# Layer norm statistics from narrow matmuls of raw tokens and of their squares, in a hybrid scan, attention and expert kernel

## The chip, the core and the metric

The kernel runs on one core of a Trainium2 chip. The metric is the device time of one execution in microseconds (us); for a kernel it is the median of several runs. A profiled execution also has a span, from the first instruction to the last. The engines are PE (TensorE: matmuls; PEld is its loading of weights), DVE (VectorE), ACT (ScalarE), POOL (GpSimd) and SP, which issues the DMAs. Everything is float32. In the profile a float32 matmul shows as two records, so 24 records are 12 matmuls of the program.

## What is computed

The input is four images of 384 channels and 32 x 32 pixels. Layer 0 is a group norm, a selective scan in four directions, a layer norm over channels and a GELU, added to the image. Layer 1 takes the 1024 pixels as tokens: a layer norm, causal attention with one head, then a layer norm and a gated mixture of four experts, of which each token uses two, each added to its input.

```python
x = x + _L0_conv_ref(_gn(x), ...)
t = _to_tokens(x)
t = t + _L1_attn_ref(_ln_t(t), Wq, Wk, Wv)
t = t + _L1_ffn_ref(_ln_t(t), gate_w, gate_b, w1, b1, w2, b2)
...
def _ln_t(v, eps=1e-5):
    m = jnp.mean(v, axis=-1, keepdims=True)
    s = jnp.var(v, axis=-1, keepdims=True)
    return (v - m) / jnp.sqrt(s + eps)
```

The norm at the end of `_L0_conv_ref` is the same over channels, with a weight and a bias, and a GELU after it.

## The kernel before

Tokens lie along the free dimension, channels on the 128 partitions in three blocks (M = 3). So a mean over channels is a matmul with `mean_w`, a matrix filled with 1/384, and its result has one number per token.

**Ticks.** The order of all instructions is written out by the program itself, in ticks. There are 768 of them for the scans (192 an image): tick t does the decay (`decay`, an Exp on ACT), the product v (`front`, L561 on DVE), the scan (`middle`, L567 on DVE), the product with C (`back`, L584 on POOL) and, every fourth tick, 16 records of y matmuls on PE (`row`, L609). In the first image many of the v products come from PE instead. `evict` (L629) takes y out of PSUM when 64 ticks of a channel block are done, into `yb`.

**Fillers.** Beside the scans of image b+1 the program places what is left of image b. `finish` (the layer norm named `l0_b`, a GELU at L888, the residual addition at L893) and `ready` (the layer norms `ff_b_0` and `ff_b_1`, one for each half of 512 tokens, and the gates) run from the list `side`; the attention and the experts (`ph`, L1272, and `fy`, L1297; L1306 and L1309 scale and add an expert's output) run from the list `waiting`. These are generators. Each `yield "pe", n` says that matmuls worth about n us were just issued; `go_on` gives the fillers 3.3 of that per tick while experts run and 4.4 while attention runs, a side generator at most until its budget of 1.0 is used up in that tick. `yield "wait", n` lets n ticks pass; `yield "inner"` resumes in the next tick but between v and the scan. What isn't issued by the last tick of the scans runs behind them. The last image's attention and experts have no scan beside them.

**Buffers.** Four PSUM banks (`banks`) and eight SBUF slots of 4 KB a partition (`slots`) are shared by all fillers; `take` waits for ticks until one is free.

**The layer norm** (`layernorm(dst, src, name, lag)`, from L639) works on n blocks of 512 tokens: n = 2 for `l0_b`, where dst and src are the same tile, n = 1 for `ff_b_h`. There are 4 of the former and 8 of the latter in a run. Its steps:

- L652: three matmuls of 128x128 by 512 for a block put the mean, repeated on all partitions, into a bank `mu`.
- L660: DVE subtracts it from the three channel blocks (128 x 1536) into dst.
- L672: ACT squares dst into three slots `sq`.
- L679: narrow matmuls (32 columns, four side by side with `tile_position`) sum the squares into the bank `var`, each group of 128 tokens on its own 32 partitions.
- L687, L692: ACT's root, then DVE's reciprocal on the narrow result `rs`.
- L698: four matmuls a block spread the narrow rows back over all partitions, into a bank `rb`.
- L708: DVE multiplies dst by it.

The attention's own norm, `scaled_tokens` (L900), has the narrow form already: raw tokens and squares go through narrow matmuls (L914), ACT squares the mean (L923), DVE subtracts (L925), then root and reciprocal (L927, L929); since its weights are centred beforehand (`fold`), only the root is spread and applied.

Of the kernel before, what the change touches and what calls it, by code (L numbers as in the profile page):

```python
# [8 lines left out]
F32 = mybir.dt.float32  # L9
AF = mybir.ActivationFunctionType  # L10
ALU = mybir.AluOpType
# [4 lines left out]
P = 128  # L16
B = 4
C = 384
M = C // P
# [30 lines left out]
def hybrid_kernel(  # L50
# [22 lines left out]
    nc = tc.nc  # L73
# [4 lines left out]
    one = ctx.enter_context(tc.tile_pool(name="one", bufs=1))  # L78
# [34 lines left out]
    inner = {}  # L113
# [4 lines left out]
    class Shared:  # L118
# [20 lines left out]
        def give(self, *names):  # L139
# [3 lines left out]
    banks = Shared(  # L143
        FIRST_BANKS,
        lambda i, name: (ps_m if i < FIRST_BANKS else pools["pm"]).tile(
            [P, 512], F32, tag=f"pm{i}", name=name
        ),
        0,
    )
    slots = Shared(  # L150
        SLOTS, lambda i, name, *shape: slotp.tile(list(shape), F32, tag=f"s{i}", name=name), 1
    )
# [7 lines left out]
    ident = const.tile([P, P], F32, tag="ident", name="ident")  # L160
    make_identity(nc, ident)
    mean_w = const.tile([P, P], F32, tag="mean_w", name="mean_w")
    nc.vector.memset(mean_w, 1.0 / C)
    eps = const.tile([P, 1], F32, tag="eps", name="eps")
# [474 lines left out]
    def layernorm(dst, src, name, lag):  # L639

        width = src.shape[2]
        n = width // 512
        mus = []
        for h in range(n):
            mu = yield from banks.take(f"mu_{name}_{h}")  # L650
            for c in range(M):
                nc.tensor.matmul(  # L652
                    mu, mean_w, src[:, c, bass.ts(h, 512)], start=(c == 0), stop=(c == M - 1)
                )
            mus.append(mu)
            yield "pe", 2.6
        yield "inner", 0
        for h in range(n):
            s = bass.ts(h, 512)
            nc.vector.tensor_tensor(  # L660
                dst[:, :, s], src[:, :, s], mus[h].unsqueeze(1).to_broadcast([P, M, 512]),
                ALU.subtract,
            )
            banks.give(f"mu_{name}_{h}")
        sqs = []
        for c in range(M):
            sq = yield from slots.take(f"sq_{name}_{c}", P, width)
            sqs.append(sq)
        for h in range(n):
            for c in range(M):  # L670
                s = bass.ts(h, 512)
                nc.scalar.activation(sqs[c][:, s], dst[:, c, s], AF.Square)  # L672
        yield "wait", lag
        var = yield from banks.take(f"var_{name}")
        for h in range(n):
            for c in range(M):
                for q in range(4):
                    o = h * 512 + q * P
                    nc.tensor.matmul(  # L679
                        var[32 * q : 32 * (q + 1), h * P : (h + 1) * P], mean_w[:, :32],  # L680
                        sqs[c][:, o : o + P], start=(c == 0), stop=(c == M - 1),
                        tile_position=(0, 32 * q),
                    )
            yield "pe", 1.0
        slots.give(*[f"sq_{name}_{c}" for c in range(M)])
        rs = one.tile([P, n, P], F32, tag=f"rs{n}", name=f"rs_{name}")
        nc.scalar.activation(  # L687
            rs, var[:, : n * P].rearrange("p (h t) -> p h t", t=P), AF.Sqrt, bias=eps
        )
        banks.give(f"var_{name}")  # L690
        yield "wait", 1
        nc.vector.reciprocal(rs, rs)  # L692
        yield "wait", lag
        backs = []
        for h in range(n):
            spread_ = yield from banks.take(f"rb_{name}_{h}")
            for q in range(4):
                nc.tensor.matmul(  # L698
                    spread_[:, q * P : (q + 1) * P],
                    ident[:, 32 * q : 32 * q + 1].to_broadcast([P, P]), rs[:, h, :],  # L700
                    start=True, stop=True,
                )
            backs.append(spread_)
            yield "pe", 1.0
        yield "inner", 0
        for h in range(n):
            s = bass.ts(h, 512)
            nc.vector.tensor_tensor(  # L708
                dst[:, :, s], dst[:, :, s], backs[h].unsqueeze(1).to_broadcast([P, M, 512]),
                ALU.mult,  # L710
            )
            banks.give(f"rb_{name}_{h}")

    folded = []

# [162 lines left out]
    def finish(b):  # L878

        yb = ybs[b]  # L880
        yield from layernorm(yb, yb, f"l0_{b}", 0)
        xrs = []
        for m in range(M):
            xr = yield from slots.take(f"xr_{b}_{m}", P, L)
            nc.sync.dma_start(xr, x[b, m * P : (m + 1) * P, :])
            xrs.append(xr)
        for m in range(M):
            nc.scalar.activation(  # L888
                yb[:, m, :], yb[:, m, :], AF.Gelu, bias=lnb[:, m : m + 1], scale=lnw[:, m : m + 1]
            )  # L890

            def add(m=m, xr=xrs[m]):
                nc.vector.tensor_add(yb[:, m, :], xr, yb[:, m, :])  # L893
                slots.give(f"xr_{b}_{m}")
                if m == M - 1:
                    finished.add(b)

            defer(1 + m // 2, add)
# [282 lines left out]
    def ready(b, h, xn, src=None):  # L1181

        if src is None:
            nc.sync.dma_start(xn, t2_d[b][:, :, bass.ts(h, 512)])
            src = xn
            yield "wait", 2
        yield from layernorm(xn, src, f"ff_{b}_{h}", 1)
        yield "wait", 1
        normed.add((b, h))
        yield from gates(b, h, xn)  # L1190
        gated.add((b, h))
# [212 lines left out]
    t = 0  # L1404
# [86 lines left out]
```

## Time and profile before

| | |
|---|---|
| median of 5 runs | 3751.58 us (3750.2 to 3755.34) |
| the profiled execution | 3754.29 us, span 3752.1 us |
| PE busy | 3356.3 us (89%) |
| DVE busy | 2961.4 us (79%) |
| ACT busy | 2086.5 us (56%) |
| POOL busy | 1817.8 us (48%) |
| mean granted TensorE clock | 0.929 |

| group | count | busy us | mean ns |
|---|---|---|---|
| L652 PE, mu of l0 | 48 | 21.7 | 594 |
| L652 PE, mu of ff | 48 | 22.3 | 596 to 601 |
| L660 DVE, subtract, both | 16 | 27.7 | 1740 to 1756 |
| L679 PE, var of l0 and ff | 384 | 14.2 | 275 to 292 |
| L698 PE, spread of l0 and ff | 128 | 19.1 | 296 to 301 |
| L708 DVE, multiply, both | 16 | 27.7 | 1746 to 1748 |
| L567 DVE, scan | 768 | 1749.2 | 2283 |
| L561 DVE, v | 664 | 841.4 | 1267 |

Matmuls are pipelined: the mean of one record is longer than the distance to the next (a 512-column record follows another after 0.43 us), and a busy PE is not PE at its peak. A wait is idle time of an engine before an instruction, put down to the instruction that released it. The clock is the share of full speed that TensorE was granted.

Three phases can be told apart. Up to 691 us the scans of image 0 run with few fillers. From there to 3098 us the scans of images 1 to 3 run with the fillers of images 0 to 2 beside them. From 3098 us on there are only the last image's norm, attention and experts, and a rest of image 2's.

### The profile page before, as it was taken

Reading aid. Unit: us, or ns where it says so; the run is one execution under the profiler, and the core shown is the slowest. Engines: PE = TensorE matmul, PEld = TensorE weight load, DVE = VectorE, ACT = ScalarE, POOL = GpSimd, SP = SyncE. Lnnn points to the kernel's source line nnn. Section 1 sums busy time; section 2 is a strip of 40 time slices with the busy share of each in tenths; the row PEclk is TensorE's granted clock in tenths of the full one; section 3 lists DMA queues with packets and bytes.
Section 4 is the critical chain, followed back from the end, with each engine's and each line's share of the span. In section 5 each row is a group of like instructions: output and inputs, shape, how many; then the busy total and the mean of one; then the engine's idle time right before and its main releaser. Section 6 shows DMA issues by size and latency. Waiting matters only on the chain. (4 is left out here: it accounts for less than half of the span.)

```text
span 3752.1 us, 35189 instructions
## 1 busy us (share of the span) xinstructions
PE 3356.3 (89%) x11891; PEld 1533.1 (41%) x11891; DVE 2961.4 (79%) x2084; ACT 2086.5 (56%) x2832; POOL 1817.8 (48%) x776
## 2 busy tenths in 40 slices
PE   4676666789999999899999999789999998999999
PEld 1333333345343343345333344354444444544444
DVE  5899899988999998989998999999999982210000
ACT  5788888556666555556655555455554552412121
POOL 2677777555565565545555665455665650000000
PEclk7777877889999999899999999999999999999999
DMA  6565555645665766436666655455656551322321
GB/s 207 211 235 198 205 210 214 227 151 191 226 228 199 256 211 232 162 137 215 225 216 231 206 203 198 145 185 185 223 191 240 181 180 38 92 79 85 95 81 53
DMA packets 408019, 680.03 MB, mean 181 GB/s; under 512 B 33520, under 2 KB 279968, under 8 KB 407840
## 3 DMA queue, kind: packets, MB, share of 16 engines
q1 hardware_dynamic: 401632, 677.40, 52.6%
q8 instruction: 94, 1.54, 0.2%
q10 hardware_dynamic: 6208, 0.39, 0.1%
q14 instruction: 85, 0.70, 0.1%
HBM read 605.16 MB, written 72.55 MB: 181 GB/s over the span
## 5 line engine op out<-in xcount | busy, mean ns | idle before, releaser
L584 POOL TENSOR_TENSOR h<-h,bc 128x1024 f32<-128x1024 f32 x768 | 1816.7, 2370 | 1270.4 <-DVE v L561 1123.3
L567 DVE TENSOR_TENSOR_SCAN h<-da,v 128x1024 f32<-128x1024 f32 x768 | 1749.2, 2283 | 56.4 <-PE v L872 25.8
L554 ACT ACTIVATE da<-dt,a 128x1024 f32<-128x1024 f32 x768 | 887.1, 1163 | 864.2 <-DVE h L567 765.1
L1297 PE MATMUL fy<-ht,w 128*128 128x512 f32 x2304 | 1022.5, 601 | 7.6 <-ACT ht L1261 5.9
L1272 PE MATMUL ph<-fx,w 128*128 128x512 f32 x2304 | 1019.6, 598 | 2.0 <-ACT dt L433 0.9
L561 DVE TENSOR_TENSOR v<-du,bc 128x1024 f32<-128x1024 f32 x664 | 841.4, 1267 | 63.0 <-DMA du<-dts 20.0
L1297 PEld LDWEIGHTS fy<-ht,w 128*128 128x128 f32 x2304 | 436.6, 192 | 581.2 <-issue 551.7
L1272 PEld LDWEIGHTS ph<-fx,w 128*128 128x128 f32 x2304 | 434.1, 191 | 578.7 <-issue 533.3
L609 PE MATMUL y<-h,sel 128*32 128x512 f32 x3072 | 496.6, 666 | 93.8 <-POOL h L584 91.8
L1257 ACT ACTIVATE ht<-ph,b1s 128x512 f32<-128x512 f32 x384 | 258.2, 680 | 479.6 <-PE ph L1272 478.1
L1306 DVE SCALAR_TENSOR_TENSOR fy<-fy,b2s,tw 128x512 f32<-128x512 f32 x96 | 72.1, 751 | 424.4 <-PE fy L1297 424.4
L609 PEld LDWEIGHTS y<-h,sel 128*32 128x32 f32 x3072 | 98.1, 116 | 405.1 <-issue 222.1
L850 ACT ACTIVATE st<-turn,bt 128x128 f32<-128x128 f32 x832 | 244.1, 553 | 0.1
L872 PE MATMUL v<-ident,st 128*128 128x128 f32 x832 | 150.3, 342 | 90.5 <-DVE h L567 89.6
L872 PEld LDWEIGHTS v<-ident,st 128*128 128x128 f32 x832 | 123.7, 178 | 132.2 <-DVE h L567 77.8
L1261 ACT ACTIVATE ht<-ht 128x3072 f32<-128x3072 f32 x64 | 177.0, 2765 | 0.8
L554 ACT ACT_TABLE_LOAD x99 | 127.0, 1283 | 18.1 <-DMA dt<-dts 11.8
L425 PE MATMUL pdt<-xd,wdt 12*128 12x512 f32 x184 | 83.7, 772 | 41.9 <-ACT dt L433 21.6
L1079 PE MATMUL po<-pt,vt 128*128 128x256 f32 x480 | 102.8, 364 | 7.2 <-ACT pt L971 7.1
L1009 PE MATMUL ss<-axn,qt 128*128 128x512 f32 (+3 forms) x288 | 101.3, 499 | 3.9 <-ACT yb L1096 3.9
L1079 PEld LDWEIGHTS po<-pt,vt 128*128 128x128 f32 x480 | 90.5, 192 | 22.3 <-ACT pt L971 10.1
L1009 PEld LDWEIGHTS ss<-axn,qt 128*128 128x128 f32 x288 | 51.3, 195 | 46.1 <-issue 32.9
(208 smaller groups left out, 1614.4 us busy)
## 6 DMA issues: line engine op xcount, KB each, us to landing
bc<-rows SPq DMA_DIRECT2D x384, 512.0 KB, 4.7
w<-in_w SPq DMA_DIRECT2D x384, 384.0 KB, 6.0
dt<-dts SPq DMA_DIRECT2D x192, 512.0 KB, 4.7
du<-dts SPq DMA_DIRECT2D x192, 512.0 KB, 6.4
dts<-dt SPq DMA_DIRECT2D x48, 512.0 KB, 4.9
dts<-du SPq DMA_DIRECT2D x48, 512.0 KB, 5.2
fx<-t2d SPq DMA_DIRECT2D x12, 768.0 KB, 5.3
tw<-mkd SPq DMA_DIRECT2D x32, 256.0 KB, 6.4
```

The source lines that it names most:

```text
L554: u["decay"] = nc.scalar.activation(u["da"], spread["dt4", n], AF.Exp, scale=a4[:, g, u["q"] : u["q"] + 1])
L561: return nc.vector.tensor_tensor(u["v"], spread["du4", n], spread["bc", n][:, 0, :], ALU.mult)
L567: nc.vector.tensor_tensor_scan(u["h"][:, ::step], u["da"][:, ::step], u["v"][:, ::step], 0.0, op0=ALU.mult, op1=ALU.add,)
L584: product = units[n]["product"] = nc.gpsimd.tensor_tensor(h, h, spread["bc", n][:, 1, :], ALU.mult)
L609: units[n]["row"] = nc.tensor.matmul(y, sel, h, start=first, stop=last, tile_position=(0, jj * DJ))
L850: nc.scalar.activation(st[:, 4 * h + t, :].rearrange("p (d i) -> p i d", i=NI)[:, i, :], ps[h][:, t * P : (t + 1) * P], AF.Copy, scale=bt[ ...
L872: nc.tensor.transpose(u["v"][:, t * P : (t + 1) * P], st[:, t, u["j"] * P : (u["j"] + 1) * P], ident)
L1079: nc.tensor.matmul(pv[:, o:], vt[:, j, m * P : (m + 1) * P], pts[step][j // 4][:, j % 4, o:], start=(alone and j == 0), stop=(j == nj - 1),)
L1257: nc.scalar.activation(ht[:, f, :], ps, AF.Identity, bias=bias)
L1261: nc.scalar.activation(ht, ht, AF.Gelu)
L1272: nc.tensor.matmul(ps, tiles[n][:, c, (f % 2) * P : (f % 2 + 1) * P], xns[h][:, c, :], start=(c == 0), stop=(c == M - 1),)
L1297: nc.tensor.matmul(pss[m], tiles[n][:, f, :], hts[fh][:, f, :], start=(fh == 0 and f == 0), stop=(fh == 1 and f == FH - 1),)
```

## The change

Mean and variance come from narrow matmuls of the raw tokens and of their squares, both into one bank. The variance is the mean of squares less the square of the mean. The narrow result is turned into the reciprocal root and its product with the mean; both are spread, and dst is src times the one less the other. The full-width mean matmuls are gone. The first square slot is kept as the place of the two narrow results until they are spread. Two banks are asked for at once for each block of 512 tokens.

Removed at the head of `layernorm`:

```diff
-        mus = []
-        for h in range(n):
-            mu = yield from banks.take(f"mu_{name}_{h}")
-            for c in range(M):
-                nc.tensor.matmul(
-                    mu, mean_w, src[:, c, bass.ts(h, 512)], start=(c == 0), stop=(c == M - 1)
-                )
-            mus.append(mu)
-            yield "pe", 2.6
-        yield "inner", 0
-        for h in range(n):
-            s = bass.ts(h, 512)
-            nc.vector.tensor_tensor(
-                dst[:, :, s], src[:, :, s], mus[h].unsqueeze(1).to_broadcast([P, M, 512]),
-                ALU.subtract,
-            )
-            banks.give(f"mu_{name}_{h}")
```

The squares and the narrow part (its old form, with `yield "pe", 1.0` a block and one root, is left out):

```diff
-                nc.scalar.activation(sqs[c][:, s], dst[:, c, s], AF.Square)
+                nc.scalar.activation(sqs[c][:, s], src[:, c, s], AF.Square)
         yield "wait", lag
...
+        w = n * P
+        for o, of in ((w, [src[:, c, :] for c in range(M)]), (0, sqs)):
+            for h in range(n):
+                for c in range(M):
+                    for q in range(4):
+                        k = h * 512 + q * P
+                        nc.tensor.matmul(
+                            var[32 * q : 32 * (q + 1), o + h * P : o + (h + 1) * P],
+                            mean_w[:, :32], of[c][:, k : k + P],
+                            start=(c == 0), stop=(c == M - 1), tile_position=(0, 32 * q),
+                        )
+                yield "pe", 0.7
+        slots.give(*[f"sq_{name}_{c}" for c in range(1, M)])
+        rs = sqs[0][:, :w]
+        mean = sqs[0][:, w : 2 * w]
+        nc.scalar.activation(rs, var[:, w : 2 * w], AF.Square)
+        yield "inner", 0
+        nc.vector.tensor_tensor(rs, var[:, :w], rs, ALU.subtract)
+        nc.scalar.activation(rs, rs, AF.Sqrt, bias=eps)
+        yield "wait", 1
+        nc.vector.reciprocal(rs, rs)
+        nc.vector.tensor_tensor(mean, var[:, w : 2 * w], rs, ALU.mult)
         banks.give(f"var_{name}")
         yield "wait", lag
```

Spreading and applying (the old form spread one row a block with `yield "pe", 1.0` and multiplied):

```diff
         for h in range(n):
             s = bass.ts(h, 512)
+            while not banks.ready(2):
+                yield "wait", 1
+            both = [banks.now(f"{x}_{name}_{h}") for x in ("rb", "mb")]
+            for x, v in zip(both, (rs, mean)):
+                for q in range(4):
+                    nc.tensor.matmul(
+                        x[:, q * P : (q + 1) * P],
+                        ident[:, 32 * q : 32 * q + 1].to_broadcast([P, P]),
+                        v[:, h * P : (h + 1) * P], start=True, stop=True,
+                    )
+            yield "pe", 1.8
+            if h == n - 1:
+                slots.give(f"sq_{name}_0")
+            yield "inner", 0
+            x, y = (v.unsqueeze(1).to_broadcast([P, M, 512]) for v in both)
+            nc.vector.tensor_tensor(dst[:, :, s], src[:, :, s], x, ALU.mult)
+            nc.vector.tensor_tensor(dst[:, :, s], dst[:, :, s], y, ALU.subtract)
+            banks.give(*[f"{x}_{name}_{h}" for x in ("rb", "mb")])
```

More of the change, by code (lines that the diff above doesn't have):

```diff
@@ L671, in layernorm @@
                 s = bass.ts(h, 512)
-                nc.scalar.activation(sqs[c][:, s], dst[:, c, s], AF.Square)
+                nc.scalar.activation(sqs[c][:, s], src[:, c, s], AF.Square)
         yield "wait", lag
         var = yield from banks.take(f"var_{name}")
[L675 to L690, printed above, removed]
+        w = n * P
[10 more added lines that the diff above has]
+                yield "pe", 0.7
@@ L691, in layernorm @@
+        slots.give(*[f"sq_{name}_{c}" for c in range(1, M)])
[5 more added lines that the diff above has]
+        nc.scalar.activation(rs, rs, AF.Sqrt, bias=eps)
         yield "wait", 1
         nc.vector.reciprocal(rs, rs)
+        nc.vector.tensor_tensor(mean, var[:, w : 2 * w], rs, ALU.mult)
+        banks.give(f"var_{name}")
@@ L693, in layernorm @@
         yield "wait", lag
[L694 to L705, printed above, removed]
         for h in range(n):
@@ L707, in layernorm @@
             s = bass.ts(h, 512)
[L708 to L712, printed above, removed]
+            while not banks.ready(2):
[8 more added lines that the diff above has]
+                    )
```

## The prediction

> **What bounds the kernel now.** I read the table of stretches first, then the waits of VectorE, then the tail in order of time. Busy columns are PE, PEld, DVE, ACT, POOL, then granted clock and DMA.
>
> ```profile
> 1496.00:1800.00 304.00, 272.57 (x1174) 137.47 (x1172) 283.61 (x224) 188.24 (x226) 157.60 (x68) 0.93 0.52 180
> 2300.00:2600.00 300.00, 269.27 (x1181) 136.66 (x1181) 288.41 (x225) 166.68 (x203) 164.79 (x70) 0.95 0.52 179
> 2850.00:3098.00 248.00, 246.68 (x748) 99.20 (x747) 231.06 (x142) 133.88 (x125) 148.13 (x63) 1.00 0.56 186
> 3098.00:3150.00 52.00, 39.59 (x238) 22.34 (x239) 22.39 (x19) 15.02 (x18) 0.00 (x0) 0.84 0.20 69
> 3150.00:3752.00 602.00, 592.84 (x1589) 283.25 (x1588) 65.66 (x131) 148.10 (x189) 0.00 (x0) 1.00 0.25 76
> ```
>
> Three regimes. The attention stretches of images 1 and 2 (first two rows, where the layer norms sit) belong to DVE: 93 to 96% busy, PE at 90%. In the expert stretches (third row) PE leads at 99%. After the last scan only PE counts, except between 3098 and 3150, where PE is idle for 12.4 us: that is the last image's norm and the start of its attention, one chain. Around the two ff norms of image 1 DVE waits almost not at all (1.5 us in 150), so whatever is added to it there delays the scans:
>
> ```profile
> DVE nb L1026 <- PE ss L1014: 0.8, 1, 0.8
> DVE nb L1026 <- PE ss L1009: 0.7, 1, 0.7
> ```
>
> The tail, from the timeline (start, duration, engine, line):
>
> ```profile
> 3098.03 1.28 DVE L629 SCALAR_TENSOR_TENSOR yb<-xe,dsum,y 128x1024 f32<-128x1024 f32 x1 [11.78 <-PE y L609]
> 3103.14 5.31 PE L652 MATMUL mu_l<-yb,mean_w 128*128 128x512 f32 x12
> 3113.53 1.52 PE L679 MATMUL var_l<-sq_l,mean_w 128*32 128x128 f32 x48
> ...
> 3120.24 1.05 PE L698 MATMUL rb_l<-rs_l,ident 128*128 128x128 f32 x8
> ...
> 3127.37 1.75 DVE L708 TENSOR_TENSOR yb<-yb,rb_l 128x1536 f32<-128x1536 f32 x1 [4.29 <-PE rb_l L698]
> ...
> 3149.30 1.98 PE L980 MATMUL pq<-axn,wg_3a 128*128 128x512 f32 x4
> ```
>
> The last y matmuls end at 3097.89 (call it T0). PE then runs, in this order, fy 5.15, mu 5.15, fy 5.15, var, fy 5.15, rb, fy 5.15, rb, with norm steps between image 2's last expert products; the first projection of image 3 starts at 3149.30, T0 + 51.4.
>
> **The change, part by part.** There are 12 norms: l0 of each image (1024 tokens, n=2) and two ff norms per image (512 tokens). Three l0 and six ff lie beside scans, one l0 and two ff in the tail.
>
> PE. An ff norm loses 6 matmul records of mu (2.58 us in the chain of waits), and gains 24 narrow ones of raw tokens (0.79 there for the 24 of the squares) and one more spread (8 records, 0.89 to 1.05): 0.8 us less. An l0 norm is twice that, 1.6. Beside scans this frees 6 x 0.8 + 3 x 1.6 = 9.6 us. The scheduler hands out PE work per tick by estimates, and a norm's estimate falls from 4.6 to 3.2 (l0 from 9.2 to 6.4), so expert products move up: in the order the changed program is built in, two fy groups are left behind the last y matmul where there were four, so 2 x 5.15 = 10.3 us now runs before T0. Net for PE before T0 +0.7, spread over 2400 us; I price it at 0. Its ends are 0 and 10.3 (the moved groups paid in full where PE leads, the freed time lying where it did not).
>
> DVE. The two wide operations per 512 tokens stay (subtract and multiply become multiply and subtract, 1.75 each), but both now run in the same place and the second needs the first. Added are a narrow subtraction and a narrow product, both reading PSUM. The attention already has this subtraction, L925, and shows its price between a product and a scan:
>
> ```profile
> 1573.81 1.23 DVE L561 TENSOR_TENSOR v<-du,bc 128x1024 f32<-128x1024 f32 x1
> 1574.95 0.42 DVE L925 TENSOR_TENSOR rs_at<-var_at,rs_at 128x256 f32<-128x256 f32 x1
> 1575.29 2.28 DVE L567 TENSOR_TENSOR_SCAN h<-da,v 128x1024 f32<-128x1024 f32 x1
> ```
>
> v ends at 1575.04, and a scan starts 0.04 after its v, so L925 put it back by 0.21. The product follows the reciprocal it needs: 0.42 + 0.04 = 0.46. The wide pair: two independent ones took 3.41 together, two dependent ones 1.75 + 0.04 + 1.75 = 3.54, about 0.15 more per pair. An l0 norm: 0.21 + 0.46 + 2 x 0.15 = 1.0. An ff norm, from the 297 ns of a 128x128 addition in PSUM (L1024): 0.10 + 0.34 + 0.15 = 0.6. Beside scans: 3 x 1.0 + 6 x 0.6 = 6.6 us. Bounds on the path: 0 and 6.6. In the expert stretches between (1000 to 1496, 1800 to 2296) DVE waited 23 and 19 us, mostly for PE, and there a late DVE only uses up slack; so I take three quarters, 5.0.
>
> The new hop. ACT must square the mean out of PSUM (373 ns, L923) before DVE subtracts; behind that subtraction stand the tick's scan, its GpSimd product and the y matmuls. ACT's root waits for DVE in turn, and behind it stand the Exp of coming ticks, held two ticks ahead. The nearest row: L925 waited for L923 in one of three images beside scans, 1.6 us. Nine norms at a third of that are 4.8; the waits that go (L660 for mu 1.4, L692 for its root 1.7) are 3.1. I take +1.0; the ends are -3.1 and 9 x 1.6 - 3.1 = 11.3. The root's table load is not new (L687 has one too). PE waits longer for a spread (0.46 more in l0); in DVE's stretches it has the room. On SP's and GpSimd's queues nothing is added: the same 1241 rows on SP, and nearly all weight loads stand two ticks or more ahead of their use, in both builds. One slot of eight is held longer, until the spreads.
>
> So T0 moves by 5.0 + 1.0 = **+6.0**.
>
> T0 to the first projection. After T0: fy 5.15 (to 5.3). DVE has yb at 1.4, ACT's six squares (0.555 apart) end at 4.8, hidden behind fy. Narrow matmuls 2 x 1.52, to 8.4. ACT's square to 8.9, table load (1.28) to 10.2, root (0.51) to 10.7, reciprocal to 12.5, product to 12.9; all under the other fy group, which ends at 13.7. Two spreads (2.1) to 15.8; four wide DVE operations to 22.9, the second spread pair beside them. From the end of L708 to the projection it was 20.2, of which 1.4 goes: L1306 and L1309 of the last fy stood between two residual additions, and are now ahead of them. First projection at T0 + 41.7, against 51.4: **-9.7**. Without that second fy group PE would wait for the chain from 8.4 to 12.9, 4.5 us.
>
> The page "ScalarE: Activation LUTs" of the Trainium skill (What ACT_TABLE_LOAD costs) adds a drain of 1.38 us to each load of 1.28. In the trace L927's root starts 1.30 after its load starts, so the sum goes without. By the rule the product would end at 14.3 instead of 12.9, 0.6 behind fy, and the tail would gain 9.1.
>
> After the projection. ff of the second half: 0.9 less on a full PE. ff of the first half: its mu ran in a gap in which PE waited for the last softmax anyway, worth nothing; var (0.79) leaves the busy part, the 0.61 wait for the reciprocal goes, one spread (1.05) comes: -0.3. Together **-1.2**; ends 0 and -3.
>
> Sum: 6.0 - 9.7 - 1.2 = -4.9, from the profiled 3752.1 us of span to 3747.2. That execution took 3754.29, 2.7 over the median; against the median 3751.58 - 4.9 = **3746.7**. A change under 0.2% (7.5 us) can't be told from none here.
>
> **The rivals.** *DVE's additions vanish* in its idle time (2273 us busy of the 2407 between 691 and 3098) and the hop costs nothing: T0 stays, 3751.6 - 10.9 = 3740.7. For it: the DVE waits for PE in expert stretches. Against: 1.5 us of wait around image 1's ff norms.
>
> *The freed PE time is worth nothing, the moved work costs its price* (the backlog shrinks on paper): T0 moves another 10.3, 3757.0. For it: PE at 99% before T0, and DVE 11.8 us early at L629. Against: work per tick is fixed by the scheduler, so full ticks stay as full.
>
> *The hop takes the place of the mean's wait*, slower: each norm's subtraction stalls DVE until ACT has squared, as L925 did once. Beyond 0.5 us on each of nine norms above my 1.0 it eats the 4.9; at 1.6 each (14.4 less the 1.0) the time is 3746.7 + 13.4 = 3760.1. For it: ACT can stand in a Gelu of 2.77 with its load of 1.28. Against: the square is issued a tick ahead, and the same hop in the attention waited once in three.
>
> **How the numbers follow.** Forecast 42%, rivals 27, 10 and 21%. The forecast's own range, 3743 to 3752, and the second rival lie within 0.2% (3744.1 to 3759.1): about 52% same, 27% faster, 21% slower. The range 3738 to 3760 takes in the first two rivals with 3 us below the first, and the edge of the third.
>
> **What would show it.** L629 of the last image near 3104, the first projection 42 us after the last y; no L652; two fy groups after the last y; narrow DVE rows of 0.3 to 0.42, 12 of each kind; the new subtraction waiting under 0.5 us on average. Wrong if L629 of the last image starts before 3099 or after 3110, or if spreads or squares show waits of several us each.

## The result, and the profile after

The changed kernel takes 3756.38 us (median of 32 runs, 3751.35 to 3761.99) against 3751.23 us before (54 runs beside them). The ratio is 1.0014, 95% interval 1.0009 to 1.0019: 5.1 us slower. That is small, but the interval lies above 1, and it is clearly not the 4.9 us faster that was forecast. The profiled execution has a span of 3753.2 us.

The stretches that answer to those of before, same columns (length, busy PE, PEld, DVE, ACT, POOL, clock, DMA):

```profile
1500.00:1800.00 300.00, 258.08 (x1243) 137.07 (x1242) 274.94 (x211) 175.10 (x215) 152.66 (x65) 0.92 0.50 178
2300.00:2600.00 300.00, 255.99 (x1256) 137.47 (x1255) 280.68 (x226) 163.71 (x204) 158.08 (x67) 0.91 0.48 168
2850.00:3110.00 260.00, 259.39 (x794) 104.72 (x793) 247.07 (x153) 140.07 (x131) 157.25 (x67) 1.00 0.58 193
3110.00:3150.00 40.00, 25.91 (x264) 18.01 (x262) 20.50 (x18) 14.18 (x17) 0.00 (x0) 0.81 0.25 89
3150.00:3753.00 603.00, 592.54 (x1643) 285.12 (x1642) 67.88 (x136) 148.62 (x191) 0.00 (x0) 1.00 0.25 76
```

In the two attention stretches (first two rows) PE has less to do, 258 of 300 us where it had 272 of 304, and DVE is no busier than before (274.94 of 300 was 283.61 of 304). Both engines idle more: something holds both. The fourth row is the tail; from L629 to the first projection it is 10.8 us shorter than before.

The tail from the timeline (start, duration, engine, line):

```profile
3109.65 1.28 DVE L629 SCALAR_TENSOR_TENSOR yb<-xe,dsum,y 128x1024 f32<-128x1024 f32 x1 [5.56 <-PE y L609]
3114.86 1.52 PE L665 MATMUL var_l<-yb,mean_w 128*32 128x128 f32 x48
3116.20 1.49 PE L665 MATMUL var_l<-sq_l,mean_w 128*32 128x128 f32 x48
3117.62 5.42 PE L1287 MATMUL fy<-ht,w 128*128 128x512 f32 x12
...
3122.87 1.05 PE L690 MATMUL rb_l<-sq_l,ident 128*128 128x128 f32 x8
...
3150.16 2.84 PE L970 MATMUL pq<-axn,wg_3a 128*128 128x512 f32 x4
```

The tail runs as the prediction drew it: narrow sums, the second fy group over the narrow chain, spreads, and the projection 40.5 us after L629 (before 51.3). The loss lies ahead of L629. All programs here are the same up to scan 192, the first of image 1, yet executions reach it at times between 673 and 682 us; so the comparison starts there. From the start of scan 192 to that of scan 767, the last, it takes 2420.2 us (before 2402.9): **+17.3**. From there to L629 -1.9, from L629 to the projection -10.8, from there to the end +0.3. The sum is +4.9.

The waits between the two scans, first PE's, then DVE's (us in total, times, longest):

```profile
PE rb_at L924 <- DVE rs_at L919: 28.0, 3, 11.7
PE var_at L904 <- DVE yb L883: 22.1, 6, 6.6
```

```profile
DVE v L561 <- PE y L609: 22.8, 9, 6.0
...
DVE sq_ff L676 <- ACT sq_ff L674: 2.9, 2, 1.7
DVE sq_ff L679 <- ACT sq_ff L677: 2.0, 2, 1.5
```

The hop that the prediction feared, L676, waited twice in nine norms. What grew belongs to no layer norm of the change: PE waits 28.0 us for the root of the *attention's* norm (rb_at, before 8.8 us in three waits), and DVE's product v waits 22.8 us for y (before 12.3). The first image's wait for rb_at is as it was (5.0, before 5.4); the second's and third's are 11.7 and 11.4 (before 1.7 each).

What the stretch between the two scans consists of, before, after, and in three experiments told of below (e8, e4, e6), with the columns as above:

```profile
681.08:3083.96 2402.88, 2276.24 (x8022) 1007.99 (x8022) 2280.65 (x1580) 1392.75 (x1482) 1356.72 (x575) 0.97 0.59 201
677.28:3097.46 2420.18, 2273.82 (x8362) 1021.29 (x8362) 2287.70 (x1597) 1399.32 (x1495) 1356.64 (x575) 0.96 0.58 200
673.39:3083.95 2410.56, 2268.48 (x8346) 1010.98 (x8346) 2287.41 (x1598) 1397.70 (x1493) 1356.98 (x575) 0.97 0.59 201
677.80:3096.02 2418.22, 2286.11 (x8022) 1011.17 (x8022) 2288.27 (x1598) 1391.91 (x1482) 1356.67 (x575) 0.96 0.59 200
674.18:3084.81 2410.63, 2284.64 (x8022) 1009.94 (x8022) 2286.05 (x1597) 1391.95 (x1482) 1355.54 (x575) 0.96 0.59 201
```

DVE's busy time grows by 7.1 us with the change (2280.65 to 2287.70): that is mostly the norm's own work. DVE's idle time, the length less the busy time, grows by 10.2 us (122.2 to 132.5): that is the larger part of the loss.

### The profile page after: what moved, and what is told of

Its sections match the earlier page's. It is cut to its first block, busy times and chain, and to the rows that moved or that the text cites. A ratio compares the mean times of both kernels' runs of the same rounds, so it can differ in the third digit from the quotient of the medians.

```text
span 3753.2 us, 36046 instructions
## 1 busy us (share of the span) xinstructions
PE 3336.5 (89%) x12307; PEld 1543.0 (41%) x12307; DVE 2971.5 (79%) x2108; ACT 2087.7 (56%) x2843; POOL 1817.6 (48%) x776
## 4 chain that ended last, share of the span: by engine, by line
PE 55%; DVE 30%; ACT 6%; issue 5%; DMA 3%; POOL 1%; SPq 1%; DVEq 0%; POOLq 0%; ACTq 0%
PE ph L1262 19%; PE fy L1287 19%; DVE h L567 16%; DVE v L561 9%; PE y L609 5%; PE pq L970 2%; PE pv L981 2%; PE po L1069 2%; PE ss L999 2%; ACT da L554 1%; DMA du<-dts 1%; ACT st L840 1%; PE pxd L392 1%; PE pdt L425 1%; POOL h L584 1%
## 5 line engine op out<-in xcount | busy, mean ns | idle before, releaser
L561 DVE TENSOR_TENSOR v<-du,bc 128x1024 f32<-128x1024 f32 x664 | 842.2, 1268 | 66.6 <-PE y L609 22.8
L609 PE MATMUL y<-h,sel 128*32 128x512 f32 x3072 | 482.1, 655 | 86.4 <-POOL h L584 84.4
L554 ACT ACT_TABLE_LOAD x99 | 127.0, 1283 | 21.5 <-DMA dt<-dts 11.7
```

Source lines behind the costliest of these rows:

```text
L554: u["decay"] = nc.scalar.activation(u["da"], spread["dt4", n], AF.Exp, scale=a4[:, g, u["q"] : u["q"] + 1])
L561: return nc.vector.tensor_tensor(u["v"], spread["du4", n], spread["bc", n][:, 0, :], ALU.mult)
L609: units[n]["row"] = nc.tensor.matmul(y, sel, h, start=first, stop=last, tile_position=(0, jj * DJ))
```

## The experiments

Each kernel ran beside the kernel before. The table gives what the readings rest on: "scans" is the time from scan 192 to scan 767, "tail" from the last L629 to the first projection of the last image, "groups" the fy groups left behind the last y, "rb_at" PE's wait for the attention norm's root. Scans, tail and groups come from one traced execution of each kernel. How far they can be trusted is seen where two programs are the same: e1 is the kernel before up to the last L629 and e2 is the changed kernel up to there, and their scans differ from those by 1.0 and 0.2 us. So a difference of about 1 us is none.

| run | scans | tail | groups | rb_at | median | ratio, 95% interval |
|---|---|---|---|---|---|---|
| before | 2402.9 | 51.3 | 4 | 8.8 | 3751.23 | |
| after | 2420.2 | 40.5 | 2 | 28.0 | 3756.38 | 1.0014 (1.0009 to 1.0019) |
| e1 | 2403.9 | 48.4 | 4 | 8.7 | 3749.23 | 1.0002 (0.9993 to 1.0011) |
| e2 | 2420.4 | 42.8 | 2 | 27.9 | 3756.44 | 1.0013 (1.0004 to 1.0022) |
| e3 | 2409.0 | 48.6 | 4 | 8.4 | 3754.55 | 1.0014 (1.0005 to 1.0023) |
| e4 | 2418.2 | 50.9 | 4 | 9.4 | 3766.20 | 1.0043 (1.0030 to 1.0056) |
| e5 | 2424.9 | 42.8 | 2 | 24.0 | 3767.37 | 1.0052 (1.0040 to 1.0065) |
| e6 | 2410.6 | 51.3 | 4 | 9.7 | 3758.03 | 1.0021 (1.0012 to 1.0030) |
| e7 | 2402.1 | 48.7 | 6 | 8.8 | 3746.17 | 0.9988 (0.9980 to 0.9997) |
| e8 | 2410.6 | 51.9 | 4 | 11.1 | 3754.69 | 1.0012 (1.0003 to 1.0021) |
| e9 | 2412.8 | 52.8 | 6 | 24.1 | 3759.21 | 1.0017 (1.0008 to 1.0026) |
| e10 | 2428.5 | 50.8 | 6 | none | 3770.26 | 1.0046 (1.0033 to 1.0058) |
| e11 | 2409.0 | 46.6 | 2 | 8.7 | 3749.52 | 0.9993 (0.9985 to 1.0002) |
| e12 | 2414.6 | 55.5 | 6 | 6.8 | 3763.70 | 1.0037 (1.0024 to 1.0050) |
| e13 | 2414.0 | 45.7 | 2 | 9.8 | 3755.09 | 1.0012 (1.0003 to 1.0021) |

**Which norms lose: e1 and e2.** The new norm in the last image alone, and in the first three alone (`<` for `==`):

```diff
+    def layernorm(dst, src, name, lag):
+        kind, b = name.split("_")[:2]
+        if int(b) == B - 1:
+            yield from layernorm_new(dst, src, name, lag)
+        else:
+            yield from layernorm_old(dst, src, name, lag)
```

> The new norm only for the last image (one l0 and two ff norms), the old one for images 0 to 2. Before is 3751.2 us, after 3756.4. All theories: the scans are as before, the last y matmuls end near 3098. Four fy groups stay behind them, and in this order (fy, narrow, fy, fy, spread, fy, spread) the first projection comes at T0 + 50.6 instead of 51.4. So 3750 us, not the 3741 that the prediction's -9.7 and -1.2 alone would give. If it is 3745 or less, the tail's gain is the new norm's own and not that of the two fy groups that moved up.

> The new norm for images 0 to 2 beside the scans, the old one for the last image. Two fy groups behind the last y as in after. All theories: the last y ends 11 to 15 us later than before, as in after; the old norm with two fy groups brings the first projection to T0 + 43, so the time is after's plus 2: 3758 us. If it is 3751 or less, the loss of after sits in the last image's norms instead.

In total e1 can't be told from before, and its tail gains only 2.9 us. e2 shows the whole loss beside the scans (+17.5) and most of the tail's gain, without a new norm in the tail. So of the 10.8 us that the tail gained, some 8 are not the norm's doing: they are two fy groups that now stand ahead of the last y.

**The work or the order: e3, e4, e6.** e3 keeps the change's instructions but gives its norms beside the scans the old length in ticks and the old charge (`old_ticks` stands for the table of the old lengths):

```diff
+        if int(name.split("_")[1]) < B - 1:
+            spare[0] -= 1.4 * n
...
+        until_ = clock[0] + old_ticks[name]
+        yield from layernorm_new(dst, src, name, lag)
+        while clock[0] < until_:
+            yield "wait", 1
```

> After, but the norms of images 0 to 2 take as many ticks as the old ones did (a wait at their end) and are charged the old 4.6 or 9.2 of PE work, so the attention starts in the old tick and four fy groups stay behind the last y, as before. Theory D (DVE's added narrow operations and their waits on ACT are what delays the scans, whatever PE does): the last y as late as in after, about 3110, and the tail back at T0 + 50.6: 3763 us. Theory P (the expert products that moved up are paid on PE before T0, and DVE waits for y matmuls behind them): the last y at 3101 to 3103, in all 3754 us.

Theory P is nearer. Beside the scans the change's own work costs +6.1 (up to L629 only +3.9, since L629 follows scan 767 2.2 us sooner than before); the other 11.2 come from the order that follows from a shorter, cheaper norm. In the total nothing of this is seen (1.0014, as the change), since four groups are back in the tail. e4 adds only DVE work to the norm before, two narrow operations that leave the value as it is:

```diff
+        nc.vector.tensor_tensor(rs, rs, rs, ALU.max)
         nc.vector.reciprocal(rs, rs)
+        nc.vector.tensor_tensor(rs, rs, rs, ALU.max)
         yield "wait", lag
```

> The kernel before with two more narrow operations on DVE in each norm (the root's result and the reciprocal, each as the larger of itself and itself, 256 or 128 columns), nothing else: same ticks, same PE order. Theory D: full price, 0.85 us in each l0 and 0.65 in each ff norm, 6.5 beside the scans and 0.9 in the last l0: 3758 us. Theory P: DVE has slack beside the scans, +1 to +3: 3753 us.

Both theories missed: +15.3 beside the scans for 6.9 us of work (three norms at 0.43 + 0.42, six at 0.44 + 0.29). e6 puts the same two operations where nobody waits for them:

```diff
+        def aside():
+            nc.vector.tensor_tensor(rs, rs, rs, ALU.max)
+            nc.vector.tensor_tensor(rs, rs, rs, ALU.max)
+
+        defer(3, aside)
```

> The kernel before, with the same two narrow VectorE operations per norm as e4 (they leave the value as it is), but issued three ticks after the norm has ended, where nothing waits for their result; PE's order and the ticks are those of before. Theory C (an operation ahead of the spread is paid twice, once on VectorE and once more through PE's in-order queue that stands behind the spread): taken out of the chain the 7.4 us cost at most their own length, 3754 to 3758. Rival (VectorE is simply full and place doesn't matter): as e4, 3764 to 3768. A second rival (they fall into VectorE's idle time): 3751 to 3753.

Now they cost +7.7, about their own length, as theory C has it (in total 3758.03, at the upper end of its range). So DVE has no slack worth the name here, and the same work ahead of a spread costs twice as much. Theory C's reason, PE's queue, is not what the waits show: in e4 DVE is idle 7.7 us longer than before, but its listed waits for PE stay at 62 us (62.0 before, 62.3 in e4, 63.8 in e6); those put down to ACT rise from 17.2 to 24.7 us, 5.6 of it in a single wait. What makes them was not isolated.

**What of the order: e5.** The old norm, with its charges laid out so that the same two fy groups move ahead of the last y (only in the first three images):

```diff
-            yield "pe", 2.6
+            yield "pe", 2.6 if last else 0.4
...
+        spare[0] -= 0.0 if last else 3.4 * n
```

> The old norm everywhere, all its instructions and its DVE work as before; only the planner's charges of the norms beside the scans are changed, so that fewer ticks pass between their steps and the same two output groups of the last expert (fy) that the change pulls ahead of the last y stand ahead of it here too (two stay behind, as after). Theory P (the two groups, 12 wide matmuls each pair of row halves, are not free ahead of T0): from scan 192 to scan 767 it takes about 11 us more than before (8 to 14), from the end of the last y to the first projection 43 (before 51.4; the old norm, two groups less), total about 3754 (3752 to 3757). Rival F (the step as the prediction had it, groups moved ahead are free, and the new norm's DVE work and hop alone make the 17 us): scans 192 to 767 take +0 to +3, total 3743 to 3746.

The tail met the expectation, the scans and the total (3767.37) neither theory: +22.0 beside the scans without any new work. Here too, PE waits 24.0 us for rs_at. What e5 shares with the changed kernel is that attention starts sooner: in the third image at tick 587 in e5 and 588 in the changed kernel, instead of 590. A row of y matmuls is issued at every fourth tick, at 589 and 593. This is PE's timeline around the third image's attention norm, before:

```profile
2379.99 2.12 PE L914 MATMUL var_at<-sq_at,mean_w 128*32 128x128 f32 x48
2381.93 1.11 PE L609 MATMUL y<-h,sel 128*32 128x512 f32 x4
2385.59 1.05 PE L609 MATMUL y<-h,sel 128*32 128x512 f32 x2 [2.56 <-POOL h L584]
2390.44 3.62 PE L609 MATMUL y<-h,sel 128*32 128x512 f32 x10 [3.81 <-POOL h L584]
2395.77 2.02 PE L934 MATMUL rb_at<-rs_at,ident 128*128 128x128 f32 x16 [1.71 <-DVE rs_at L929]
```

and after:

```profile
2378.26 2.72 PE L904 MATMUL var_at<-sq_at,mean_w 128*32 128x128 f32 x48
2380.80 1.89 PE L609 MATMUL y<-h,sel 128*32 128x512 f32 x16
2394.06 3.70 PE L924 MATMUL rb_at<-rs_at,ident 128*128 128x128 f32 x16 [11.37 <-DVE rs_at L919]
```

PE ran its matmuls in the order in which the program issued them. Before, a row of y was issued while the norm's narrow chain ran on ACT and DVE, and its matmuls were done as h came. After, the chain starts two ticks sooner; the row that is ready (2380.80) is through at once, the next stands behind rb_at, and PE is idle for 11.37 us. That row, done by 2394 before, starts at 2405.88, behind three of attention's projections too.

**The place of attention: e8, e9, e10, e12.** e8 is the changed kernel with attention held to its old ticks, e9 the kernel before with attention two ticks later (`!= 0`):

```diff
-        while b not in finished:
+        while b not in finished or b < B - 1 and clock[0] % 4 != 2:
```

> The changed kernel with one line different: attention of the first three images starts at a tick that leaves 2 over from a division by 4, which is where it started before the change (206, 398, 590; with the change 205, 396, 588). A row of y matmuls is issued at every tick that leaves 1 over; held so, the spread of attention's own norm (rb_at) is issued just behind such a row, as before, and not two ticks ahead of it. Theory A (place of rb_at): PE's waits for rs_at fall from 28.0 us to 8 to 10, VectorE's for y from 22.8 to 9 to 13, scans 192 to 767 from 2420.2 to 2406 to 2411, total 3751 to 3755 (four groups stay behind the last y, so the tail gives 8 back). Rival D (the new norm's VectorE work and its extra hop are what costs beside the scans): scans 2417 or more, total 3760 or more.

> The kernel before, old norm, with attention of the first three images held two ticks longer, so that it starts at a tick divisible by 4, the place that the change gave it; nothing else is changed, and six output groups stay behind the last y instead of four. Theory A: rb_at stands ahead of a row of y matmuls again, PE waits 20 to 30 us for rs_at (before 8.8), VectorE waits 18 us or more for y (before 12.3), scans 192 to 767 take 2409 to 2417 (before 2402.9), total 3755 to 3762. Rival G (what costs is output groups pulled ahead of the last y): two groups more stay behind, so the scans take 2402 or less, total 3745 to 3750.

Both came out about as theory A has it: e8 takes 9.6 us off the scans and rb_at's wait falls to 11.1 (forecast 8 to 10); e9, with no new instruction and two groups *fewer* ahead of the last y, loses 9.9 and waits 24.1. e9's timeline at the same place:

```profile
2389.82 0.27 PE L914 MATMUL var_at<-sq_at,mean_w 128*32 128x128 f32 x1
2399.11 3.78 PE L934 MATMUL rb_at<-rs_at,ident 128*128 128x128 f32 x16 [9.01 <-DVE rs_at L929]
```

The wait for rb_at is not itself the price: in e8 PE's wait for h ahead of the rows rises from 30.3 to 54.5 us, and PE idles 142.1 us where it idled 146.4 in the changed kernel. What falls is DVE's idle time, to 123.2 us, 0.9 over before (third row of the five above); its busy time stays 6.8 over before. e8's total is hardly better than the changed kernel's: four groups stay behind, and its tail is 11.4 longer. Two further runs tried how far the place alone explains. e10 holds only the spread, e12 holds attention of the kernel before by a whole period of the rows:

```diff
+        while b < B - 1 and clock[0] % 4 != 1:
+            yield "wait", 1
         backs = []
```

```diff
-        while b not in finished:
+        while b not in finished or clock[0] < (210, 402, 594, 0)[b]:
```

> The changed kernel, attention starting as early as it does there, but the spread of attention's norm alone (rb_at and what follows it) is held until the tick at which a row of y matmuls has just been issued. Six groups stay behind the last y. Theory A, its narrow form (it is the place of rb_at in PE's queue, not the start of attention): rb_at's wait at 10 or less, scans 192 to 767 2404 to 2411, total 3747 to 3753. Its wide form (attention two ticks early is itself what costs): scans 2415 or more, total 3756 or more.

> The kernel before, old norm, with attention of the first three images held four ticks (210, 402, 594 instead of 206, 398, 590), a whole period of the rows of y, so that rb_at stands just behind a row again; six groups stay behind the last y, as in e9. Theory A (place against the rows of y, period four ticks): rb_at's wait at 6 to 12, VectorE's wait for y at 9 to 15, scans 192 to 767 2400 to 2408, total 3745 to 3752. Rival L (every tick of delay of attention costs, or moves it against other work too, so e10's slowness comes from standing four ticks later): scans 2415 to 2428, total 3760 to 3770.

In both, rb_at stands behind a row again and waits little or not at all, as e12's list of PE's waits shows (its first line before was 35.9 us):

```profile
PE y L609 <- POOL h L584: 56.1, 29, 3.8
PE ph L1272 <- DMA w<-in_w: 9.3, 2, 5.9
PE var_at L914 <- ACT sq_at L905: 7.1, 8, 2.2
PE rb_at L934 <- DVE rs_at L929: 6.8, 3, 2.5
```

and both are slow, +25.6 and +11.7 beside the scans; e12's total, 3763.70, is in rival L's range. In e10 the third image's spread stood six ticks later than after (tick 597 instead of 591), since the hold missed a tick in the first image and everything behind it slid. So theory A is right that the wait for rs_at is made by the place against the rows, and wrong that this place is all that a shift of attention changes. A delay by four ticks costs about as much by other waits (in e12 DVE waits 26.1 us for attention's scores, before 16.7), and which of them decides was not settled. Nor does e10 test its narrow form cleanly, as attention itself starts later in it (in the third image at tick 592, after at 588).

**The two groups: e7, e11, e13.** e11 is the kernel before with a pace of 3.4 instead of 3.3 from tick 626, e13 is e8 with 3.35 there; both leave two groups behind. e7 is e1 with a charge that leaves six:

```diff
+        if name == "ff_2_1":
+            pace[0] = 3.4
```

```diff
+        if name == "ff_2_1":
+            spare[0] -= 8.0
```

> e1 (the new norm in the last image alone) with one charge of 8 to the filler's budget at the last norm beside the third image's scans, so that six output groups instead of four stay behind the last y. Theory P turned round: each group taken away ahead of T0 is worth about 5.6 us there and costs about 4 behind it: scans 192 to 767 some 11 us shorter than e1's (2393), last y to first projection 56 (e1 48.4), total 3746 (3743 to 3749). Rival F (fillers ahead of T0 are free): scans as e1, tail +8, total 3757.

> The kernel before with the filler's pace in the last stretch beside the scans (third image's experts, from tick 626) raised from 3.3 to 3.4, so that two output groups stay behind the last y instead of four, and attention's places are those of before in all three images. Theory G: the scans from 192 to 767 take 11 us more (2414), the tail from last y to first projection 43 instead of 51, total 3754. Theory A (the two groups themselves cost little ahead of the last y): scans +1 to +4 (2404 to 2407), tail 43, total 3744 to 3748.

> e8 (the changed kernel with attention at its old ticks) with the filler's pace from tick 626 raised from 3.3 to 3.35, so that two output groups stay behind the last y, exactly those of the changed kernel. Theory A+G (e8's place is worth some 5 us before the last y, and moving two groups up costs about what the tail gives back): scans 192 to 767 2412 to 2418, last y to first projection 41 to 44, total 3750 to 3755. Rival G (the two groups are the whole difference between e8 and the changed kernel): scans 2420, total 3756 to 3758.

e11: the two groups cost 6.1 beside the scans, between the two expectations; 3.1 come back between scan 767 and L629 and 4.7 in the tail, so the total can't be told from before. e13 has the changed kernel's instructions and two groups behind, with attention at its old ticks: its scans take 2414.0, 3.4 more than e8's and 6.2 less than the changed kernel's.

But both missed the forecast tail of about 43 (46.6 and 45.7), and from scan 192 to the end e13 takes as long as the changed kernel (3076.0 and 3075.9). The two groups that stay behind stand elsewhere. In the changed kernel the second one runs while ACT and DVE work on the norm's narrow sums; in e13 it runs ahead of the second half of the sums, and PE waits for the spread:

```profile
3114.14 5.42 PE L1289 MATMUL fy<-ht,w 128*128 128x512 f32 x12
3119.49 1.52 PE L667 MATMUL var_l<-sq_l,mean_w 128*32 128x128 f32 x48
3125.18 2.08 PE L692 MATMUL rb_l<-sq_l,ident 128*128 128x128 f32 x8 [4.17 <-DVE sq_l L681]
```

The wait of 4.17 us, and 2.08 for a spread that took 1.05 in the changed kernel, make up nearly all of the 5.2 us by which e13's tail is longer. So how a loss or gain is divided depends on where the count stops, and the place of attention alone is not shown to be worth anything in the total.

e7's total is as forecast, but not for the reason given: the scans hardly shorten (-1.8, little more than the spread of equal programs), L629 follows scan 767 3.0 sooner than in e1, and the tail takes two more groups for nothing (48.7 against e1's 48.4). It is the one version that beats both kernels, by 0.12% (0.03 to 0.20) against before; as the best of thirteen its interval flatters it.

## Why the prediction was wrong

- **"Net for PE before T0 +0.7 ... I price it at 0": this step failed.** By e3 the order that comes with the shorter, cheaper norm costs 17.3 - 6.1 = 11.2 beside the scans, a little over the upper end of 10.3, and 11.5 up to L629. The groups were counted, but the prediction treated "moved" as PE time that could be made up, and of attention's earlier start, one or two ticks, the step said nothing: a shorter norm moves everything gated by `finished`, not only fillers. By e8 and e13 the 17.3 fall into 7.7 for the norm's own work and hop, 3.4 for the two groups (6.1 in e11) and 6.2 for attention's earlier start. Up to L629 the same runs give 2.5, 7.5 and 5.4. So that the order costs is shown; how much of it is the groups and how much attention's place is not.
- **The freed PE time** (9.6 us) bought nothing: PE's busy time between the scans fell by 2.4 us, its idle time rose by 19.7.
- **T0 by DVE's work and the hop, +6.0:** about right beside the scans, 6.1 in e3 and 7.7 in e8. Up to L629, where T0 is, it is less, 3.9 and 2.5: DVE's wait for PE ahead of L629, 11.78 us before, is 9.64 and 6.62 there, so part of the delay falls into that wait. DVE's busy time grew by 7.1, near the 6.6 at full price; the discount to three quarters for slack in the expert stretches has no support, as e6 paid 7.7 us for 6.9. The hop's own rows gave 4.8 - 3.1 = 1.7, of which it took 1.0; the waits L676 and L679 less those of before (1.7 and 1.4) make +1.8.
- **Tail, -9.7:** right, -10.8 from L629. But 8 of it is the price of the failed step seen from the other side: the groups' gain was booked here and their cost at 0. The 4.5 us that PE would wait without the second group over the narrow chain came out in e13, 4.17.
- **After the projection, -1.2:** measured +0.3, which decides nothing. Kernels with the same norm there take 603.1 (after, e1, e3) to 606.6 us (e7, e8), those with the old one 601.2 (e2) to 606.4 (e12). No gain is seen.
- **Rivals.** The second ("the moved work costs its price") gave 3757.0 and is nearest, 0.6 off, in part by luck: it has the groups' price but nothing of attention's place. The third, the hop, is ruled out: 2.9 us of waits for L674 in all, where it needed 14.4. The first is ruled out by e3 and e6.
- **Signs named in advance:** two groups behind the last y and no L652, the narrow rows at 0.29 to 0.42, the projection 41 us after L629: seen. L629 "near 3104" came at 3109.65, just short of the 3110 that was to mean wrong. But this execution reached scan 192 3.8 us sooner than the one before; counted from there L629 is 15.4 later, which on the clock of before would be about 3113. So that sign, too, says wrong. SP issues 1436 DMAs in each of the two traces, not 1241; that the number is the same, which was what counted, holds.

What stays open is why attention up to two ticks sooner, two later and four later all cost 6 to 12 us beside the scans: the place before the change is the best of those tried there, and no single wait explains the others.

## What to carry to other kernels

Where a program fixes the order of its queues by its own clock, making one step shorter is a change of order for all that stands behind it; run that order with the old work (as e5 and e9 do) before crediting the work that was saved. If a gain behind a boundary comes from work that moved ahead of it, book both sides at a price, not one of them at zero. Time freed on an engine that wasn't the bound was worth nothing here, and a small operation on the engine that was cost about its length where nobody waited for it (e6) and twice that ahead of a matmul that did (e4).

## What the runs showed of the hardware

Work put into a hole can be nearly free, in part by the clock. The attention norm's 96 narrow matmul records in the tail, before, after, and in e7, whose two extra groups fill the gap ahead of them:

```profile
3133.00:3141.00 8.00, 5.60 (x96) 4.08 (x96) 3.62 (x4) 3.96 (x4) 0.00 (x0) 0.50 0.57 191
```

```profile
3135.00:3142.00 7.00, 5.51 (x96) 4.13 (x96) 2.74 (x3) 4.33 (x5) 0.00 (x0) 0.52 0.03 12
```

```profile
3129.00:3133.00 4.00, 3.63 (x99) 2.60 (x97) 2.31 (x3) 1.46 (x3) 0.00 (x0) 1.00 0.17 62
```

After 5.7 us without work (9.0 in the changed kernel) PE was granted about half its clock, 0.50 and 0.52, and the records took from 3133.0 to 3141.2 and from 3135.6 to 3142.1, also because they came as DVE gave them their tokens. In e7 PE came straight from fy, was granted 1.00, and took 2.8 us (3129.8 to 3132.6). The slow spread of e13, after its wait of 4.17 us, is another case:

```profile
3125.18:3127.00 1.82, 1.82 (x8) 1.82 (x9) 0.41 (x1) 0.00 (x0) 0.00 (x0) 0.50 0.99 230
```

The Trainium skill agrees ("TensorE: Matmul & The Clock Gate", Part 1: The HAM clock gate): one idle window of about 3.4 us halves the rate, and it comes back after about as long a busy one. The idle times here, 4.17 to 9.0 us, are all longer than that; no run here measures the window itself.
